# Fewer and larger DMAs for the head sums and the decays of a chunked state-space stage

## The chip, the cores and the metric

One core of one Trainium2 chip runs the whole program in one launch. The metric is the device time of that launch in microseconds. The engines are named as in the profile: PE (TensorE) for matmuls, DVE (VectorE), ACT (ScalarE), POOL (GpSimd), and SP (SyncE), whose queue issues nearly all DMAs.

## What is computed

The program is four layers in a row on `x` of 4 x 512 x 256, each adding to `x` what it makes of a layer norm of `x`: a Mamba scan, a mixture of experts (MoE), a chunked state-space layer (SSD), and the same MoE again. The change touches the SSD layer alone, which is, cut to what matters:

```python
dA  = (dt * A).reshape(b, c, 32, 64)            # 64 heads, 8 numbers each
Acs = jnp.cumsum(dA, axis=2)
Lm  = jnp.exp(_segsum(dA))                      # within a chunk: exp(Acs[l] - Acs[s]), l >= s
Y_diag = einsum('bclhn,bcshn,bchls,bcshp->bclhp', Ch, Bh, Lm, xd)
states = einsum('bclhn,bclh,bclhp->bchpn', Bh, exp(Acs[-1] - Acs), xd)
prev   = scan over chunks: h = h * exp(Acs[-1]) + states
Y_off  = einsum('bclhn,bchpn,bclh->bclhp', Ch, prev, exp(Acs))
y = rms_norm(Y_diag + Y_off) * silu(z) @ W_out
```

`Acs`, the running sums of a head within a chunk of 32 tokens, are the "head sums" (`cs`). `exp(Acs[-1])`, the factor by which a state shrinks over a chunk, are the "decays".

## The kernel before

A program in two parts writes itself. `block` records every operation in a list (`Plan.note`), with its tiles; `Plan.order` then places them: a list scheduler with a price for every operation picks, engine by engine, the ready operation of the highest rank; 24 such orders are made and the one whose replay is shortest is emitted. Every instruction therefore carries line 612 (`emit`) in the profile (table loads carry line 610), and is told apart by the names of its tiles. Each engine runs its instructions in the order emitted and waits where an operand is not ready. So a change to a few DMAs changes the order of the whole program a little.

The SSD layer runs over four batches b of 512 tokens. 16 blocks of 32 tokens make the chunks; the 64 heads are taken in four groups g of 16, a group in four quads q of four heads, and two groups make a pair p. For each batch:

- `front_a` and `front_b` (lines 1507 to 1708) make the projections, the head sums (bank `pcs`, copied to `c_s`), and `over_blocks`, the decays of each head over blocks. Each of the two halves of `c_s` (`a` = 0, 1: 32 heads, each in a high and a low part, 64 rows of 512) is stored to DRAM tensor `cs_rows` (line 1664). The decays go to `dk_rows`, 64 heads of 128 numbers (line 1680). A head's row in `dk_rows` is its decays over 16 blocks, repeated for its 8 numbers.
- `weighted` (lines 1775 to 1799) makes for one group the weighted inputs `xw` and `xe` on POOL, stores `xw` to `x_rows`, and loads the group's head sums back from `cs_rows` into one of four buffers `less`, as rows k (block) by q, h, s: eight DMAs a group, one for each of the two parts and four quads (lines 1791 to 1798).
- `apart` (lines 1801 to 1809) loads `x_rows` back, spread by blocks, into one of two buffers `x_b`, in four DMAs a group.
- `decayed` (lines 1870 to 1884): matmul `pe` of `less` and `c_s`, exponential on ACT, mask on DVE or POOL: tile `m`. `within` (lines 1886 to 1899): 32 x 16 small matmuls `pz` of `m` and `x_b` a group; the group before the one that `decayed` works on.
- `states` (lines 1811 to 1868), once a pair: matmuls `pst` into `starts`, two scans on DVE (one each for h = 0, 1, the half of a group's heads), then matmuls `po_s_p`. Each scan reads a tile `decays` of 128 partitions x 1024: 64 partitions for each group of the pair, each row the same 4 KB of `dk_rows`. It is loaded by two DMAs of 64 partitions, one for each group (lines 1822 to 1825). `decays` has two buffers, so a pair's two loads wait for the scans of the pair before.

All these DMAs are issued on SP, one after another, in the planner's order. SP also waits in that order: an issue whose data is not there holds everything behind it. The DMAs take turns on eight completion semaphores, so that an issue also waits until the DMA eight places ahead has landed.

Of the kernel before, what the change touches and what calls it, by code (L numbers as in the profile page):

```python
# [22 lines left out]
F32 = mybir.dt.float32  # L23
# [15 lines left out]
DI, NH, HD, DS = 512, 64, 8, 64  # L39
# [16 lines left out]
BL, NB = 32, P // 32  # L56
# [14 lines left out]
def bc(ap, axis, n):  # L71

    a = ap.unsqueeze(axis)
    shape = list(a.shape)
    shape[axis] = n
    return a.to_broadcast(shape)
# [641 lines left out]
def block(ctx: ExitStack, tc: Plan, a: dict, out: bass.AP):  # L718
# [929 lines left out]
    def front_b(b):  # L1648

        nm, small, rot, d_a, zs, xs, wt, ld = made_a.pop(b)  # L1650

        pcs = bank(FRONT_BANKS if b == 0 else "mm", f"pcs_{nm}")
        for i in range(NT):
            T.matmul(
                pcs[:, i * P : (i + 1) * P], d_a[:, i].rearrange("p a c h -> p (a c h)"), upto_b,
                start=True, stop=True,
            )
        cs_rows = dram.tile([2, NH, L], F32, tag="cs_rows", name=f"cs_rows_{nm}")
        cs = c_s[b % 2]
        for a in range(2):  # L1660
            src, lo = pcs[a * NH : (a + 1) * NH], a * NH + NH // 2
            S.copy(cs[a][NH:], src)
            V.tensor_tensor(cs[a][NH + NH // 2 :], pcs[lo : lo + NH // 2], cs[a][NH + NH // 2 :].bitcast(F32), ALU.subtract)
            nc.sync.dma_start(out=cs_rows[a], in_=cs[a][NH:].bitcast(F32))
            V.tensor_copy(
                tot[b % 2][a * NH // 2 : (a + 1) * NH // 2, 1:],
                src[: NH // 2].rearrange("p (k l) -> p k l", l=BL)[:, :-1, BL - 1],
            )

        pc = bank(FRONT_BANKS if b == 0 else "mm", f"pc_{nm}")  # L1670
        T.matmul(pc[:, : L // 2], upto_b, d_a[:, :, :, 0, :], start=True, stop=True)
        T.matmul(pc[:, L // 2 :], after_b, d_a[:, :, :, 0, :], start=True, stop=True)
        ends = s_o.tile([P, 2, NT, NH], F32, tag="ends", name=f"ends_{nm}")
        S.activation(ends.rearrange("p c i h -> p (c i h)"), pc, AF.Exp)

        nk = NT * NB
        over_blocks = small("over_blocks", (NH, HD, nk))
        S.activation(over_blocks, bc(tot[b % 2], 1, HD), AF.Exp)
        dk_rows = dram.tile([NH, HD * nk], F32, tag="dk_rows", name=f"dk_rows_{nm}")
        nc.sync.dma_start(out=dk_rows, in_=over_blocks.rearrange("p d k -> p (d k)"))  # L1680
        yield


        nh = NT * NB // 2
        bt = small("rest", (P, L))
        cm = c_m[b % 2]
        for g in range(2):
            pt = bank(FRONT_BANKS if b == 0 else "mm", f"pbc_{nm}_{g}")
            for i in range(NT):
                T.transpose(pt[:, i * P : (i + 1) * P], rot[:, i, g].rearrange("p c n -> p (c n)"), ident)  # L1690
            S.copy(bt if g == 0 else cm, pt)
        bm = b_m[b % 2]
        S.copy(bm, rot[:, :, 0, 0, :])
        gm = s_o.tile([P, nh, 2, BL], F32, tag="gm", name=f"gm_{nm}")
        pg = bank(FRONT_BANKS if b == 0 else "mm", f"pg_{nm}")
        for k in range(nk):
            ks = slice(k * BL, (k + 1) * BL)
            for h in range(4):
                T.matmul(pg[h * BL : (h + 1) * BL, ks], bt[:, ks], cm[:, ks], start=True, stop=True)
        S.activation(gm.rearrange("p j c l -> p (j c l)"), pg, AF.Copy, scale=0.5)  # L1700
        dg = small("tsin", (P, NT, DS))
        V.tensor_tensor(dg, rot[:, :, 0, 0, :], rot[:, :, 1, 0, :], ALU.mult)
        dd = small("dd", (P, NT))
        V.tensor_reduce(dd, dg, AX.X, ALU.add)
        V.tensor_tensor(ld, ld, bc(dd, 2, NH), ALU.mult)
        ready[b] = dict(
            nm=nm, zs=zs, y=xs, wt=wt, ld=ld, ends=ends, dk_rows=dk_rows, gm=gm, cm=cm, bm=bm, cs=cs, cs_rows=cs_rows
        )
# [66 lines left out]
    def weighted(b, g):  # L1775

        c = ready[b]
        nm = f"{c['nm']}_{g}"
        ch, hs = slice(g * P, (g + 1) * P), slice(g * 16, (g + 1) * 16)
        xs = c["y"][:, :, ch]  # L1780
        xw = pool2.tile([P, NT, P], F32, tag="xw", name=f"xw_{nm}", bufs=1)
        G.tensor_tensor(per_head(xw), per_head(xs), bc(c["wt"][:, :, hs], 3, HD), ALU.mult)
        x_rows = dram.tile([L, P], F32, tag="x_rows", name=f"x_rows_{nm}", bufs=4)
        nc.sync.dma_start(out=x_rows.rearrange("(i p) f -> p i f", p=P), in_=xw)
        xe = pool2.tile([P, NT, P], F32, tag="xe", name=f"xe_{nm}", bufs=XE_BUFS)
        G.tensor_tensor(per_head(xe), per_head(xw), bc(c["ends"][:, 1, :, hs], 3, HD), ALU.mult)

        G.tensor_tensor(per_head(xs), per_head(xs), bc(c["ld"][:, :, hs], 3, HD), ALU.mult)
        nk = NT * NB
        ls = less[g]  # L1790
        for part in range(2):
            for q in range(4):
                lo = part * NH // 2 + g % 2 * 16
                src = c["cs_rows"][g // 2, lo + q : lo + 16 : 4, :]
                nc.sync.dma_start(
                    out=ls[part * nk : (part + 1) * nk, q, :].bitcast(F32).rearrange("k (h s) -> k h s", h=4),
                    in_=src.rearrange("h (k s) -> k h s", s=BL),
                )
        units[b, g] = dict(xe=xe, x_rows=x_rows, less=ls)

    def apart(b, g):
# [9 lines left out]
    def states(b, p):  # L1811

        c = ready[b]
        nm = f"{c['nm']}_p{p}"
        nk = NT * NB
        pair = (2 * p, 2 * p + 1)
        half = [slice(h * DS, (h + 1) * DS) for h in range(2)]
        G.memset(starts[:, :, 0], 0.0)
        decays = []
        for h in range(2):  # L1820
            t = pool2.tile([P, P // 2 * nk], F32, tag="decays", name=f"decays_{nm}_{h}")
            for j, g in enumerate(pair):
                at = 16 * g + 8 * h
                src = c["dk_rows"][at : at + 8, :].rearrange("h d -> (h d)")
                nc.sync.dma_start(out=t[half[j]], in_=src.partition_broadcast(DS))
            decays.append(t)


        for r0 in range(0, NB, 2):
            pts = [bank("c", f"pst_{nm}_{r0 + r}", (P, NT, P)) for r in range(2)]  # L1830
            tc.chain = []
            for i in range(NT):
                for r in range(r0, r0 + 2):
                    if i * NB + r + 1 == nk:
                        continue
                    rs = slice(r * BL, (r + 1) * BL)
                    for j, g in enumerate(pair):
                        T.matmul(
                            pts[r - r0][half[j], i, :], c["bm"][rs, i, :], units[b, g]["xe"][rs, i, :],
                            start=True, stop=True,  # L1840
                        )
            tc.chain = None
            for r in range(r0, r0 + 2):
                n = NT if r + 1 < NB else NT - 1
                at = starts[:, :, r + 1 : r + 2 + NB * (n - 1) : NB]
                S.copy(at.rearrange("p c i -> p i c"), pts[r - r0][:, :n, :])
            yield
        for h in range(2):
            at = starts[:, h * P // 2 : (h + 1) * P // 2, :].rearrange("p c k -> p (c k)")
            V.tensor_tensor_scan(at, decays[h], at, 0.0, ALU.mult, ALU.add)  # L1850
        yield
        po = [bank("c", f"po_{nm}_{j}", (P, NT, P)) for j in range(2)]
        tc.chain = []
        for k in range(nk):
            for j in range(2):
                r = slice(k % NB * BL, (k % NB + 1) * BL)
                T.matmul(
                    po[j][r, k // NB, :], c["cm"][half[j], k * BL : (k + 1) * BL], starts[half[j], :, k],
                    start=True, stop=True,
                )  # L1860
        tc.chain = None
        for j, g in enumerate(pair):
            hs = slice(g * 16, (g + 1) * 16)
            off = pool2.tile([P, NT, P], F32, tag="off", name=f"off_{nm}_{j}")
            V.tensor_tensor(per_head(off), per_head(po[j]), bc(c["ends"][:, 0, :, hs], 3, HD), ALU.mult)
            y = c["y"][:, :, g * P : (g + 1) * P]
            G.tensor_tensor(y, y, off, ALU.add)
        yield
# [176 lines left out]
```

## Time and profile before

| | |
|---|---|
| median of 3 runs | 846.15 us (842.12 to 849.16) |
| the profiled execution | 836.37 us, of it 834.7 us from the first to the last instruction |
| busy, share of that span | PE 85%, DVE 82%, ACT 63%, POOL 63% |
| the SSD stage by its batches, us of the span | 440 to 505, 505 to 572, 572 to 640, 640 to 712 |
| DMA share of the 16 engines in these four | 0.42, 0.31, 0.32, 0.57 |
| DMAs in the stage for head sums | 8 stores (2 a batch), 128 loads of 8 KB |
| DMAs in the stage for decays | 4 stores, 32 loads of 256 KB |

The page's table of groups gives an engine's busy time for one operation and its mean; its table of DMA issues gives the number, the size and the median time from issue to landing. The chain of work is followed back from the last instruction of the program: "SPq" in it is time in which the SP queue was issuing a DMA that the chain stood behind.

### The profile page before, as it was taken

The numbers are of one execution on the slowest core, as the hardware profiler recorded it, in microseconds if no ns is written. First come the engines' busy times: TensorE is split into PE (matmuls) and PEld (weight loads), VectorE is DVE, ScalarE is ACT, GpSimd is POOL, SyncE is SP. The second block draws the span as 40 slices with busy tenths as digits, with TensorE's granted clock in tenths as the row PEclk, the third lists the DMA queues.
The fourth block names the chain that finished last, engine by engine and source line by source line (L and its number), as shares of the span: only waits on it lengthen the run. The fifth ranks groups of instructions, "written<-read, shape, count | busy, mean of one in ns | idle before, by whom it ended". The sixth has DMA issues, their size and how long they took to land.

```text
span 834.7 us, 16400 instructions
## 1 busy us (share of the span) xinstructions
PE 709.5 (85%) x6194; PEld 457.5 (55%) x6194; DVE 683.8 (82%) x1278; ACT 523.4 (63%) x965; POOL 527.2 (63%) x410
## 2 busy tenths in 40 slices
PE   8889879966676789799997697789789886999996
PEld 5333324221022247587886475676567664888784
DVE  7488999999999984898996678697677546799987
ACT  2898976865345486566687455645636544686764
POOL 5735857767767574655555886863862873558555
PEclk9989999976577699999999599899789778999999
DMA  8321252241341002600004522521531584000001
GB/s 273 117 76 64 71 184 64 92 162 64 101 176 51 1 7 57 273 1 0 2 5 112 116 64 60 112 65 38 117 80 32 131 264 101 1 1 26 25 2 51
DMA packets 79247, 67.55 MB, mean 81 GB/s; under 512 B 48696, under 2 KB 66040, under 8 KB 78400
## 3 DMA queue, kind: packets, MB, share of 16 engines
q1 hardware_dynamic: 77664, 65.35, 27.2%
q10 hardware_dynamic: 1504, 1.15, 0.5%
q8 instruction: 49, 0.80, 0.4%
q14 instruction: 30, 0.25, 0.1%
HBM read 49.67 MB, written 16.80 MB: 80 GB/s over the span
## 4 chain that ended last, share of the span: by engine, by line
PE 35%; DVE 15%; ACT 8%; SPq 5%; issue 5%; POOL 3%; DMA 1%; POOLq 0%; ACTq 0%; DVEq 0%
PE ph_e L612 8%; PE ph_f L612 6%; SPq L612 5%; PE pz_s L612 4%; DVE hs L612 3%; PE px_s L612 3%; PE po_s L612 2%; DVE starts L612 2%; PE pst_s_p L612 2%; DVE bx L612 1%; PE po_s_p L612 1%; ACT L610 1%; ACT ph_e L612 1%; PE pe_s L612 1%; DVE ph_f L612 1%
## 5 line engine op out<-in xcount | busy, mean ns | idle before, releaser
L612 POOL TENSOR_TENSOR hs<-hs,cb 128x1024 f32<-128x1024 f32 x64 | 151.8, 2380 | 73.8 <-DVE hs L612 61.1
L612 DVE TENSOR_TENSOR_SCAN hs<-da,bx 128x512 f32<-128x512 f32 x128 | 150.5, 1213 | 8.3 <-ACT da L612 5.8
L612 ACT ACTIVATE da<-ds,a_neg 128x512 f32<-128x512 f32 x128 | 87.5, 689 | 76.8 <-DVE hs L612 76.6
L612 PE MATMUL ys<-hs,over 128*32 128x512 f32 x256 | 73.7, 755 | 27.9 <-POOL hs L612 27.9
L612 DVE TENSOR_TENSOR bx<-us,pb 128x1024 f32<-128x1024 f32 x64 | 76.3, 1211 | 0.2
L612 POOL TENSOR_TENSOR m_s<-m_s,gm_s 128x512 f32<-128x512 f32 x32 | 45.3, 1421 | 32.8 <-ACT m_s L612 32.7
L610 ACT ACT_TABLE_LOAD x51 | 65.4, 1283 | 0.9
L612 PE MATMUL pconv<-hh,conv 128*128 128x512 f32 x128 | 60.8, 622 | 1.1 <-ACT hh L612 1.1
L612 ACT ACTIVATE ph_f<-ph_f 128x512 f32<-128x512 f32 x64 | 37.5, 588 | 26.9 <-DVE ph_f L612 26.6
L612 DVE TENSOR_TENSOR ph_f<-ph_f,expert_b 128x512 f32<-128x512 f32 x64 | 43.9, 694 | 11.7 <-DMA expert_b<-in_expert_b_dram 5.7
L612 ACT ACTIVATE ph_e<-ph_e 128x512 f32<-128x512 f32 x64 | 36.8, 586 | 23.7 <-DVE ph_e L612 15.9
L612 PE MATMUL ph_e<-expert_h,xs_of_xh_e 128*128 128x512 f32 x128 | 44.9, 413 | 4.2 <-ACT c_e L612 4.2
L612 PE MATMUL pe_s<-c_s,less 128*128 128x512 f32 x64 | 32.9, 544 | 16.2 <-DMA less<-cs_rows_s 7.4
L612 PEld LDWEIGHTS ys<-hs,over 128*32 128x32 f32 x256 | 8.8, 118 | 66.9 <-POOL hs L612 51.9
L612 POOL TENSOR_TENSOR c_e<-c_e,hb_e 128x512 f32<-128x512 f32 x16 | 20.6, 1290 | 36.1 <-ACT hb_e L612 36.1
L612 PEld LDWEIGHTS pconv<-hh,conv 128*128 128x128 f32 x128 | 24.1, 196 | 34.4 <-issue 28.1
L612 ACT COPY starts<-pst_s_p 128x512 f32<-128x512 f32 (+1 forms) x32 | 29.6, 1010 | 18.3 <-PE pst_s_p L612 18.3
L612 PE MATMUL pz_s<-x_b,m_s 128*32 128x32 f32 x2048 | 31.9, 216 | 10.0 <-DMA x_b<-x_rows_s 5.7
L612 DVE TENSOR_TENSOR_SCAN starts<-decays_s_p,starts 128x1024 f32<-128x1024 f32 x16 | 38.9, 2439 | 1.5 <-issue 1.3
L612 PEld LDWEIGHTS pz_s<-x_b,m_s 128*32 128x32 f32 x2048 | 26.3, 127 | 23.4 <-issue 15.3
L612 PE MATMUL ph_f<-expert_h,xh_f 128*128 128x512 f32 x96 | 38.4, 400 | 0.7 <-ACT c_f L612 0.7
L612 PE MATMUL ph_f<-expert_l,xh_f 128*128 128x512 f32 x96 | 38.4, 400 | 0.0
(399 smaller groups left out, 2163.2 us busy)
## 6 DMA issues: line engine op xcount, KB each, us to landing
decays_s_p<-dk_rows_s SPq DMA_DIRECT2D x32, 256.0 KB, 4.3
ds<-d_rows SPq DMA_DIRECT2D x14, 512.0 KB, 3.8
us<-u_rows SPq DMA_DIRECT2D x14, 512.0 KB, 3.9
cb<-c_rows SPq DMA_DIRECT2D x16, 256.0 KB, 3.3
x_rows_s<-xw_s SPq DMA_DIRECT2D x16, 256.0 KB, 3.0
x_b<-x_rows_s SPq DMA_DIRECT2D x64, 64.0 KB, 2.4
x<-in_x_dram SPq DMA_DIRECT2D x4, 512.0 KB, 4.7
raw_expert<-in_expert_w_dram SPq DMA_DIRECT2D x4, 512.0 KB, 7.1
```

The costliest lines, as they stand in the source:

```text
L610: self.real.scalar.preload_act_table_set(n.table)
L612: n.inst = f(*[self.swap(v) for v in n.args], **{k: self.swap(v) for k, v in n.kw.items()})
```

## The change

The head sums of a half are stored in four DMAs of 16 rows instead of one of 64; within each 16 rows the order in DRAM becomes quad by quad, head by head, which is the order in which `less` wants them. A group's `less` is then loaded by one DMA for each part, 16 blocks x 16 heads = 256 rows of 32 numbers, instead of four of 64 rows. A pair's decays for one h come by one DMA for both groups instead of two.

```diff
-            nc.sync.dma_start(out=cs_rows[a], in_=cs[a][NH:].bitcast(F32))
+            for at in range(0, NH, 16):
+                nc.sync.dma_start(
+                    out=cs_rows[a, at : at + 16].rearrange("(q h) l -> h q l", h=4),
+                    in_=cs[a][NH + at : NH + at + 16].bitcast(F32),
+                )
...
         for part in range(2):
-            for q in range(4):
-                lo = part * NH // 2 + g % 2 * 16
-                src = c["cs_rows"][g // 2, lo + q : lo + 16 : 4, :]
-                nc.sync.dma_start(
-                    out=ls[part * nk : (part + 1) * nk, q, :].bitcast(F32).rearrange("k (h s) -> k h s", h=4),
-                    in_=src.rearrange("h (k s) -> k h s", s=BL),
-                )
+            lo = part * NH // 2 + g % 2 * 16
+            nc.sync.dma_start(
+                out=ls[part * nk : (part + 1) * nk].bitcast(F32).rearrange("k q (h s) -> k (q h) s", s=BL),
+                in_=c["cs_rows"][g // 2, lo : lo + 16, :].rearrange("h (k s) -> k h s", s=BL),
+            )
...
-            for j, g in enumerate(pair):
-                at = 16 * g + 8 * h
-                src = c["dk_rows"][at : at + 8, :].rearrange("h d -> (h d)")
-                nc.sync.dma_start(out=t[half[j]], in_=src.partition_broadcast(DS))
+            src = c["dk_rows"].rearrange("(g c h) d -> g c (h d)", c=2, h=8)[2 * p : 2 * p + 2, h]
+            nc.sync.dma_start(out=t, in_=bc(src, 1, DS))
             decays.append(t)
```

As the built programs have it, outermost dimension first: a load of decays had 64 rows of 1024 on both sides, the source with a step of zero; now its destination is 128 rows of 1024 and its source is 2 x 64 (a step of zero) x 1024. A load of `less` was 16 x 4 x 32 and is 16 x 16 x 32. A store of head sums was 64 x 512 on both sides; now its source is 16 x 512 and its destination 4 x 4 x 512.

## The prediction

> **What bounds the kernel now.** I read the page's chain first, then the chain cut to the SSD stage, its waits, and the DMA tables. The chain's share for SP stands out, since SP computes nothing:
>
> ```profile
> PE 35%; DVE 15%; ACT 8%; SPq 5%; issue 5%; POOL 3%; DMA 1%; POOLq 0%; ACTq 0%; DVEq 0%
> ```
>
> The chain cut to 440 to 712 us puts the whole of it into the stage that is changed, 16.6% of 272 us = 45 us, and cut to 577 to 606 us it is nearly alone:
>
> ```profile
> by line: SPq L612 80.9%; DMA x_b<-x_rows_s 8.5%; issue 7.8%; PE pe_s L612 2.5%; PE pz_s L612 1.2%
> ```
>
> There SP issues DMA after DMA (the timeline of SP), some 0.5 us each, until the fourth `x_b` of group 2 has gone at 602.5:
>
> ```profile
> 586.00 3.87 SPq L612 DMA_DIRECT2D less<-cs_rows_s  x6
> 589.98 1.96 SPq L612 DMA_DIRECT2D x_b<-x_rows_s  x4
> 591.99 2.39 SPq L612 DMA_DIRECT2D less<-cs_rows_s  x3
> 594.42 1.11 SPq L612 DMA_DIRECT2D decays_s_p<-dk_rows_s  x2
> 595.62 0.53 SPq L612 DMA_DIRECT2D x_rows_s<-xw_s  x1
> 596.20 2.02 SPq L612 DMA_DIRECT2D less<-cs_rows_s  x4
> 598.26 1.09 SPq L612 DMA_DIRECT2D decays_s_p<-dk_rows_s  x2
> 599.40 1.32 SPq L612 DMA_DIRECT2D less<-cs_rows_s  x1
> 600.82 2.21 SPq L612 DMA_DIRECT2D x_b<-x_rows_s  x4
> ```
>
> What PE pays is read from the stage's waits on PE (total, times, longest):
>
> ```profile
> PE pe_s L612 <- DMA less<-cs_rows_s: 7.4, 4, 5.8
> PE pz_s L612 <- DMA x_b<-x_rows_s: 5.7, 3, 2.9
> ```
>
> 13.1 us in all; the rest of the 45 us runs beside PE, which is busy for 222 of the 272. Then the DMAs themselves (number, KB, median us from issue to landing):
>
> ```profile
> decays_s_p<-dk_rows_s SPq DMA_DIRECT2D x32, 256.0 KB, 4.3
> x_rows_s<-xw_s SPq DMA_DIRECT2D x16, 256.0 KB, 3.0
> x_b<-x_rows_s SPq DMA_DIRECT2D x64, 64.0 KB, 2.4
> less<-cs_rows_s SPq DMA_DIRECT2D x128, 8.0 KB, 2.8
> ```
>
> Two more rows carry the forecast. `less` landed in 2.7 us at the median and 14.3 at most (minimum, median, maximum):
>
> ```profile
> DMA to landing us min/median/max: 1.6/2.7/14.3
> ```
>
> The late ones were issued from 667 on, behind two 2 MB loads of expert weights (665.55 and 666.59): a transfer waits for what was queued on the same DMA engines before it. And a stretch in which these loads keep all 16 busy gives the rate of one (columns end with DMA share and GB/s):
>
> ```profile
> 669.00:677.00 8.00, 7.90 (x127) 6.24 (x114) 4.71 (x8) 4.32 (x9) 7.84 (x9) 1.00 1.01 397
> ```
>
> 397 / 16 = 24.8 GB/s for one engine.
>
> **The change part by part.** *Loads of head sums, 128 to 32.* A load of `less` holds SP for 0.6 us on average (the timeline's 77.3 us for 128). 64 rows or the 512 rows of an `x_b` cost SP about the same (medians 0.43 and 0.49), so one of 256 does too; landing 2.4 to 2.8 by the same two rows. *Stores, 8 to 32*, at 0.47: 24 more. *Loads of decays, 32 to 16*, at 0.57. Together 88 issues fewer, some 50 us of the queue's time, between 0 us (all beside other work) and 45 us (all that the chain shows) of the program's. I take the 13.1 us that PE waited: the nearest row, since PE's order is fixed and it pays only when it stands.
>
> *How a load of decays is spread.* It moves 512 KB now, and its source has 2 as the outermost dimension. The trace keeps every update of a DMA's semaphore. All DMAs of SP have 16, which I read as one for each engine that took part, but two: `raw_bias` and `bias`, the only ones of 4 rows, have five: for `raw_bias` one as the issue ends (24.15 us) and four at landing (25.05, 25.07, 25.14, 25.37). So a DMA of 4 rows ran on 4 engines, while those with 16, 32 or 64 outermost ran on 16. No row has 128 on one side and 2 on the other. Bounds: 16 engines, landing as now, 4.3 us; 2 engines, 256 KB each at 24.8 GB/s = 10.6 us, and 21.2 for a pair's two if they use the same two engines. I take the second: the nearest row is the one with a small outermost dimension. The stores (destination 4 x 4) would run on 4 engines with four rows of 2 KB each, as many per engine as 64 rows on 16: nothing.
>
> *The Trainium skill*, "DMA: Bandwidth & Descriptors", "Rules for kernel authors", speaks on both sides: it tells one to coalesce many small transfers, and it says that an outermost dimension below 16 on either side confines the DMA to at most that many engines. By the first alone the time would be 833 us; by the second, which gives two engines here, 890. The five updates agree with the second.
>
> *What stands behind the decays.* Every other DMA of SP has rows on those two engines and waits for its share there, as `less` did for 14.3 us. In the order of the built program, in batches 1 and 2 a pair's first two loads stand ahead of `x_b` of group 1 (in batch 2 also of its `x_rows`). Batch 2, counted from its first store of head sums (574.8 before): 20 issues at 0.5 put the first load at +10, with the two engines taken from about +11 to +32. `x_rows` of group 1 lands at +33; four issues and 2.4 us put `x_b` at +37.5, where it was +19.7. `xw` has one buffer, so `x_rows` of group 2 follows then: issue +35.5, landing 3.0, four issues, 2.4: +43, where PE had it at 605.1, +30.3. **13 us late**, and PE's matmuls behind it stand in fixed order. Batch 1: the decays cannot go before `dk_rows` (issued at 523.4, +18, behind ACT) has landed, +20; engines taken to +42; `x_rows` of group 2, issued meanwhile, lands at about +43.5, `x_b` at +48 for 537.7, +32.3: **16 late**. Batch 0: the second load stands just ahead of the first `x_b`: 10.6 us on its two engines, less 3, since seven loads of `less` stood around that `x_rows` (458.2 to 463.5 us) and two do now: **7**. Batch 3 (from 643.3): the second pair's two loads stand ahead of `x_b` of group 2, and wait for the first pair's scans, which ended at 668.5, +25, and come 21 later; so they take the engines from +47 to +68, and that `x_b` lands at +69 for +50 (691.3 and 2.4); against these 19 the late `less` of group 3 goes (PE's wait of 5.8 us), as all `less` now go ahead of or between the expert weights: **13**. In each batch PE stands at `pz`; behind it in PE's order are the last quads' `pe`, `pst`, `po_s_p` and the next batch's projections, and DVE, ACT and POOL wait for these. Sum 49 us, with the gain on SP already in it as it is counted by issues. Off it go 5 us for waits of PE that end while it stands anyway (PE idles 10 to 14 us in each batch).
>
> *The scans.* The two scans of a pair came 12 to 39 us after its first load was issued; the second load would land at 23. The short ones are first pairs, which are later anyway; nothing added.
>
> *The order of the rest.* In Mamba and the first MoE the built orders differ in places; DVE is busy for 232 of the 240 us from 50 to 290, so a better order has little to win and I take 0, with 4 us either way.
>
> Sum: 836.4 + 49 - 5 = 880 us for an execution like the profiled one. The median of the runs stands 9.8 us above that execution, so the forecast is **890 us**.
>
> **Rivals.** *A, the loads use all 16 engines.* For: 128 destination rows. Against: the 4-row DMAs. Then only SP's gain is left: 846 - 13 = 833 us, faster. It decides at about 3 us of exposed delay a batch, which is decays landing in some 6 us instead of 4.3, six engines or more.
>
> *B, two engines, but only the scans wait.* If other DMAs pass the two busy engines, the second scan of each pair stands only where its load lands after 23 us: the distances were 24, 39, 20.5, 22.6, 22, 22, 12 and 23, so 17 us, less 13: 850 us. Against: the 14.3.
>
> *C, the blocks are exposed in full.* If nothing covers the first pairs' 21.2 us and each second pair holds back some 5: 4 x 26 - 13 = 91: 937 us. For: within a batch PE has little to do that needs no `x_b`. Against: 10 to 14 us of idle PE a batch.
>
> *D, the queue is not relieved*, because the eight completion semaphores hold SP instead: a part of C.
>
> **How the numbers follow.** Forecast 0.62, A 0.13, B 0.10, C with D 0.15. The forecast's own range is 861 (846 + 24.5 - 5 - 4: half of the 49 covered, and the order's 4) to 931 (846 + 73.5 - 5 + 17: half as much again, and the scans). With B and C the range is 850 to 940. A and the tails, 2 in 10, are left out. 1% is about what a measurement of this kernel can tell from no change: faster A, 0.12; within 1% most of B, 0.08; slower 0.80.
>
> **What would show it.** Right: decays land in 12 to 25 us; the DMA share falls while PE waits for `x_b` for 10 us or more a batch; `x_b` or `x_rows` land in over 10 us after the decays; SPq nearly gone from the chain of issues that follow one another, with DMA in its place; the stage's 272 us become some 315. Wrong: decays land in 4 to 6 us (A), or land late while `x_b` keeps 2.4 us (B).

## The result, and the profile after

| | before | after |
|---|---|---|
| median of 6 runs each | 844.31 us (839.11 to 849.16) | 912.51 us (906.92 to 917.16) |
| ratio, 95% interval | | 1.080 (1.0745 to 1.086) |
| profiled execution, its span | 836.37, 834.7 us | 914.04, 912.3 us |
| DMAs in the stage for head sums and decays | 136 and 36 | 64 and 20 |
| mean granted TensorE clock | 0.894 | 0.844 |

The change made the kernel 68 us slower. The forecast was 890 us, in a range of 850 to 940. The page's chain of the kernel after, by engine:

```profile
PE 34%; DMA 11%; DVE 10%; POOL 8%; issue 5%; ACT 4%; SPq 3%; POOLq 0%; DVEq 0%; ACTq 0%
```

Against the chain shown of before, SP's queue fell from 5% to 3%, DMA rose from 1% to 11% and POOL from 3% to 8%. The chain cut to the stage, of before (440 to 712 us) and of after (440 to 800 us), names the DMAs:

```profile
by line: SPq L612 16.6%; PE pz_s L612 10.7%; issue 8.0%; PE px_s L612 5.8%; PE po_s L612 5.4%; DVE starts L612 5.1%; PE pst_s_p L612 4.9%; PE po_s_p L612 4.2%; PE pe_s L612 3.2%; PE ph_f L612 2.0%; DMA x_b<-x_rows_s 1.8%; DVE m_s L612 1.7%;
by line: DMA x_rows_s<-xw_s 15.3%; issue 9.3%; DMA decays_s_p<-dk_rows_s 9.1%; SPq L612 7.9%; PE pz_s L612 5.0%; POOL m_s L612 4.8%; DVE starts L612 4.6%; PE px_s L612 3.0%; POOL zs_s L612 2.9%; PE pst_s_p L612 2.6%; PE pe_s L612 2.2%; DVE 
```

24% of 360 us are two kinds of transfers that are not among the costliest parts of the chain before: the stores `x_rows` and the loads of decays. SP's queue in the stage's chain went from 45 to 28 us. What the engines waited for in the same window (total, times, longest), first PE, then POOL, then DVE:

```profile
PE pz_s L612 <- DMA x_b<-x_rows_s: 44.7, 4, 17.4
PE pyt_s L612 <- POOL zs_s L612: 17.3, 1, 17.3
PE pz_s L612 <- POOL m_s L612: 11.9, 6, 5.7
```

```profile
POOL xw_s L612 <- DMA x_rows_s<-xw_s: 63.8, 6, 20.9
```

```profile
DVE starts L612 <- DMA decays_s_p<-dk_rows_s: 12.3, 3, 9.0
```

The prediction had PE pay through `x_b`, which is the largest line. It used the one buffer of `xw` to delay the next `x_rows`, but it did not count what else POOL holds back meanwhile. POOL stood 64 us (4.7 before) because `xw` has one buffer and the next `xw` needs the store of the last one landed.

Batch 0 as SP issued it (start, time, what, how many):

```profile
463.83 0.56 SPq L612 DMA_DIRECT2D decays_s_p<-dk_rows_s  x1
...
465.00 0.38 SPq L612 DMA_DIRECT2D x_rows_s<-xw_s  x1
...
474.03 0.52 SPq L612 DMA_DIRECT2D decays_s_p<-dk_rows_s  x1
477.91 7.79 SPq L612 DMA_DIRECT2D x_b<-x_rows_s  x4
485.81 3.35 SPq L612 DMA_DIRECT2D x_rows_s<-xw_s  x1
...
491.26 2.57 SPq L612 DMA_DIRECT2D x_b<-x_rows_s  x4
```

The landings are read from the updates of each DMA's semaphore. The first load of decays, issued at 463.83, landed 12.88 us later, at 476.7. `x_rows`, issued 1.2 us behind it, had 14 of its 16 updates within 3.1 us and the last two at 12.8 and 12.9. The second load (474.03) landed after 15.32 us, at 489.35; the first `x_b`, issued at 477.91, had 14 of 16 within 2.2 us and the last two at 11.7 and 11.9. Two parts of sixteen were late each time, as many as the engines of the decays.

SP's queue was held as well. Of the four `x_b` at 477.91 the third took SP 5.44 us to issue (479.74), where 0.49 is usual, although the DMA eight places ahead of it had landed at 477.2; in batch 1 two such issues, at 546.30 and 555.86, took 9.5 and 5.2 us with no wait for a semaphore in them:

```profile
543.76 17.85 SPq L612 DMA_DIRECT2D x_b<-x_rows_s  x4
```

What holds an issue is not shown. From a batch's first store of head sums to the end of the last `pz`, SP's issues took 141 us for 267 DMAs before and 175 us for 179 after, of which 12.9 us were a wait for PE. In batch 0 this lies on the chain: the `x_rows` at 485.81 could go only when the four `x_b` had been issued.

The chain in batch 2 shows what the late parts cost. There a store waits behind both loads of its pair, and the second pair's second scan behind its load:

```profile
621.47 2.52 POOL m_s L612 x2
623.99 22.01 DMA x_rows_s<-xw_s
646.13 1.07 POOL xw_s L612
...
671.40 2.25 DVE starts L612
673.67 15.63 DMA decays_s_p<-dk_rows_s
689.32 2.29 DVE starts L612
```

The stage in the parts of its four batches (length, then busy time of PE, PEld, DVE, ACT, POOL with counts, granted clock, DMA share, GB/s):

```profile
451.00:529.00 78.00, 51.37 (x838) 37.78 (x836) 49.74 (x87) 35.87 (x68) 46.84 (x38) 0.74 0.31 82
529.00:609.00 80.00, 58.64 (x1128) 45.03 (x1128) 53.96 (x83) 36.71 (x69) 39.81 (x34) 0.83 0.23 59
609.00:697.00 88.00, 62.39 (x1039) 46.47 (x1039) 48.76 (x78) 39.58 (x73) 40.06 (x34) 0.82 0.21 56
697.00:782.00 85.00, 52.85 (x1129) 41.70 (x1129) 31.44 (x57) 30.12 (x52) 35.96 (x33) 0.66 0.41 129
```

PE was busy for 225 us of these 331, as it was for 221 of the 270 before: the stage holds nearly the same work and 57 us more of standing. The DMA engines are busy for 21 to 31% in the first three batches (31 to 42% before) while PE waits for DMA: a mean over 16 engines does not show that two of them are full.

### The profile page after: what moved, and what is told of

Read it like the earlier page. It is cut to its first block, busy times and chain, and to the rows that moved or that the text cites. A ratio compares the mean times of both kernels' runs of the same rounds, so it can differ in the third digit from the quotient of the medians.

```text
span 912.3 us, 16289 instructions
## 1 busy us (share of the span) xinstructions
PE 735.2 (81%) x6194; PEld 472.9 (52%) x6194; DVE 683.7 (75%) x1278; ACT 516.2 (57%) x959; POOL 524.4 (57%) x410
## 4 chain that ended last, share of the span: by engine, by line
PE 34%; DMA 11%; DVE 10%; POOL 8%; issue 5%; ACT 4%; SPq 3%; POOLq 0%; DVEq 0%; ACTq 0%
PE ph_e L612 10%; PE ph_f L612 9%; DMA x_rows_s<-xw_s 6%; DMA decays_s_p<-dk_rows_s 4%; SPq L612 3%; PE pz_s L612 2%; DVE hs L612 2%; POOL m_s L612 2%; DVE starts L612 2%; PE px_s L612 2%; DVE bx L612 1%; PE po_s L612 1%; POOL zs_s L612 1%; PE pst_s_p L612 1%; PE ys L612 1%
## 5 line engine op out<-in xcount | busy, mean ns | idle before, releaser
L612 PE MATMUL pz_s<-x_b,m_s 128*32 128x32 f32 x2048 | 33.0, 222 | 57.5 <-DMA x_b<-x_rows_s 44.7
L612 POOL TENSOR_TENSOR m_s<-m_s,gm_s 128x512 f32<-128x512 f32 x32 | 42.0, 1323 | 46.0 <-ACT m_s L612 46.0
L612 POOL TENSOR_TENSOR xw_s<-xs_s,wt_s 128x512 f32<-128x512 f32 x16 | 17.7, 1106 | 85.3 <-DMA x_rows_s<-xw_s 63.8
L612 DVE TENSOR_TENSOR m_s<-pe_s,gm_s 128x512 f32<-128x512 f32 x32 | 21.8, 683 | 43.9 <-PE pz_s L612 36.1
L612 ACT ACTIVATE ph_f<-ph_f 128x512 f32<-128x512 f32 x64 | 37.2, 590 | 21.6 <-DVE ph_f L612 21.2
```

Of the source, the lines that this page charges most:

```text
L612: n.inst = f(*[self.swap(v) for v in n.args], **{k: self.swap(v) for k, v in n.kw.items()})
```

## The experiments

Lengths of batches below go from a batch's first store of head sums to the next one's, the last to the end of the last `pz`, each from the trace of one execution.

**Only one thing changed: on how many engines a load runs.** The kernel before, with the source of its 64-row loads of decays written as 2 x 32, 4 x 16 or 8 x 8 (steps of zero). Number, size and order of the instructions stay.

```diff
-                nc.sync.dma_start(out=t[half[j]], in_=src.partition_broadcast(DS))
+                nc.sync.dma_start(out=t[half[j]], in_=bc(bc(src, 0, 32), 0, 2))
```

> The kernel before with one thing changed: the source of each load of decays (64 rows with a step of zero) is written as 2 x 32 with steps of zero. Every engine's order of instructions, the number of DMAs and their bytes (32 loads of 256 KB) stay as they are. Theory (engines as many as the outermost dimension): each load runs on two engines, 128 KB each at 24.8 GB/s, 5.3 us and 21 for the four of a pair on the same two, so nearly the whole loss comes: 885 to 930 us. Rival (order of the program, size of a load, number of DMAs): 838 to 848 us, as before.

> The same with 4 x 16 as the source: four engines, 64 KB each, 2.6 us a load and 10.6 for a pair's four. Theory: the block is half as long and part of it is hidden: 850 to 875 us. Rival: 838 to 848 us.

> The same with 8 x 8 as the source: eight engines, 32 KB each, 1.3 us a load, 5.3 for a pair's four. Theory: a load lands in some 4 to 6 us, and what is left is hidden: 840 to 852 us. Rival: 838 to 848 us, which this run alone does not tell apart; it is for where the loss begins.

| source of a load | 64 (before) | 8 x 8 | 4 x 16 | 2 x 32 |
|---|---|---|---|---|
| time, us | 839.3 | 850.4 | 865.9 | 914.4 |
| ratio, 95% interval | 1 | 1.014 (1.009 to 1.018) | 1.034 (1.028 to 1.040) | 1.090 (1.085 to 1.095) |
| updates of its semaphore | 16 | 9 | 5 | 3 |
| landing, us: minimum, median, maximum | 3.3, 4.2, 7.7 | 4.2, 5.9, 9.8 | 5.5, 8.6, 12.7 | 8.8, 13.7, 23.2 |
| lengths of the batches, us | 68.7, 69.4, 68.5, 63.5 | 76.4, 70.0, 71.7, 66.0 | 75.8, 76.0, 75.0, 70.0 | 86.4, 83.9, 86.8, 90.0 |

This is the run that settles the cause. With every engine's order as before, the form of a source alone brings 75 us, and the loss grows as the engines become fewer. The updates are one more than the engines: with 2, 4 and 8 outermost one update comes as the issue ends, the others at landing. The Trainium skill, "DMA: Bandwidth & Descriptors", "Why a DMA increments its semaphore by 16 and not by 1", says the same: the issuing queue writes the missing part at once, and each engine that takes part adds one as its data lands; the counts 3, 5 and 9 agree. In batch 0 the four loads of the first pair, issued within 1.8 us, landed 9.1, 14.3, 19.8 and 25.0 us after the first was issued: steps of 5.2, 5.5 and 5.1 us, against 5.3 worked out from 128 KB at 24.8 GB/s. They use the same two engines, one behind the other. On four engines the four loads landed 3.3, 2.5 and 2.6 us apart (64 KB at that rate take 2.6). On eight it was 2.2, 2.8 and 2.1, where 32 KB would take 1.3: there the rate of an engine no longer gives the step, and what does is not shown. The chain of the 2 x 32 kernel, cut to the stage (436 to 784 us):

```profile
by line: DMA decays_s_p<-dk_rows_s 26.3%; issue 7.1%; SPq L612 6.7%; DMA x_rows_s<-xw_s 5.7%; PE pz_s L612 4.4%; DMA expert_l<-kept_expert_l 3.8%; DMA moe_rows<-kept_rows 3.5%; DVE starts L612 2.8%; PE pe_s L612 2.5%; PE px_s L612 2.1%; PE 
```

**Either part of the change alone.** Head sums as changed with the decays in two loads again, and the decays as changed with the head sums as before:

```diff
-            src = c["dk_rows"].rearrange("(g c h) d -> g c (h d)", c=2, h=8)[2 * p : 2 * p + 2, h]
-            nc.sync.dma_start(out=t, in_=bc(src, 1, DS))
+            for j, g in enumerate(pair):
+                at = 16 * g + 8 * h
+                src = c["dk_rows"][at : at + 8, :].rearrange("h d -> (h d)")
+                nc.sync.dma_start(out=t[half[j]], in_=src.partition_broadcast(DS))
```

> The head sums' part of the change alone: stores by quads and one load of 256 rows for four of 64, while the decays keep two loads of 64 partitions. Theory (the two-engine decays cost all of it): the gain on SP is left, at most the 13.1 us that PE waited and what of the 45 us of SP's queue more: 815 to 840 us, ratio to before 0.97 to 0.995. Rival (the new order of the program, its later start of the SSD stage by 14.8 us, or the stores on four engines make it slow): 860 to 915 us, and batches of the stage as long as with the whole change.

Measured 830.5 us, ratio 0.987 (0.983 to 0.992): 1.3% below the kernel before, a small gain but clear of the noise, and the shortest time of this study.

> The decays' part of the change alone: one load of 512 KB for a pair and h, source 2 x 64 x 1024; head sums as before. Theory (two engines, and other transfers behind them): slower about as much as the whole change, +50 to +85 us, 895 to 930 us, as SP is relieved of only 16 issues; decays land 12 to 22 us after their issue and x_b behind them. Rival (order of the program or the stores): 840 to 850 us.

Measured 926.8 us, ratio 1.102 (1.0975 to 1.106), loads landing in 12.1 to 22.2 us. The two ratios multiply to 1.088 beside 1.080 for the whole: the parts hardly act on each other. The Trainium skill has a rule for this very edit ("DMA: Bandwidth & Descriptors", "Rules for kernel authors"): of two transfers to disjoint halves of the partitions it would make one over 128. Here that cost 86 us (0.102 of 841.3), because the one transfer had 2 as its source's outermost dimension; the page's rule on that dimension is the one that decided. In the kernel with the head sums alone, what PE waited for over its whole stage:

```profile
PE pz_s L612 <- DMA x_b<-x_rows_s: 2.4, 2, 1.4
...
PE pe_s L612 <- DMA less<-cs_rows_s: 2.2, 1, 2.2
```

Before, these two lines were 5.7 and 7.4 us.

**One load for both groups, on sixteen engines.** The decays are written to DRAM in eight copies, so that the source of the 512 KB load is 16 x 8 (step of zero) x 1024:

```diff
-        nc.sync.dma_start(out=dk_rows, in_=over_blocks.rearrange("p d k -> p (d k)"))
+        for g in range(4):
+            nc.sync.dma_start(
+                out=dk_rows[g].rearrange("r h d -> h r d"),
+                in_=bc(over_blocks[16 * g : 16 * g + 16].rearrange("p d k -> p (d k)"), 1, 8),
+            )
...
-            nc.sync.dma_start(out=t, in_=bc(src, 1, DS))
+            nc.sync.dma_start(out=t, in_=bc(src, 1, 8))
```

> The whole change, but the decays of a pair and h are written to DRAM in eight copies, so that the one load of 512 KB has 16 as the outermost dimension of its source (16 x 8 with a step of zero x 1024) and the number of DMAs for loading stays at 16. The four stores of copies (128 rows each) are added per batch. Theory (the number of engines decides): 16 engines, 815 to 845 us, decays landing in 4 to 6 us. Rival (the size of 512 KB, or one DMA where there were two, makes the wait): 890 to 915 us, as with the change.

Measured 844.8 us, ratio 1.003 (0.9995 to 1.006); loads land in 4.5, 5.1 and 10.5 us (minimum, median, maximum). The size of a load and the number of loads are not what costs 8%. It stays 14 us above the head sums alone, and why was not settled: twelve more stores, loads that land 0.6 us later and another order of the whole program came together.

**The decays on another queue.** ACT issues them instead of SP, still on two engines:

```diff
-            nc.sync.dma_start(out=t, in_=bc(src, 1, DS))
+            nc.scalar.dma_start(out=t, in_=bc(src, 1, DS))
```

> The whole change, but the decays' loads are issued on ACT's queue instead of SP's; they still run on two engines. Two ways in which others can stand behind them: if a transfer waits only behind what its own queue put on the same engine, x_rows and x_b on SP's queue pass the decays, and what is left is the scans' wait and sharing of two engines: 840 to 875 us. If any transfer on the two engines waits whatever queue it came by: 890 to 920 us.

Measured 901.4 us, ratio 1.073 (1.066 to 1.081). That is in the range of the second expectation, but neither has the mechanism. Four loads `x_b` that SP issued beside decays that ACT issued at 566.95 and 572.51:

```profile
570.10 1.90 SPq L612 DMA_DIRECT2D x_b<-x_rows_s  x4
```

The four landed at 580.0, 585.3, 590.7 and 591.4, each with 14 of 16 updates within 3.6 us of its issue and two late; the decays landed at 580.7 and 591.2. A DMA of one queue does not stand behind the whole of what the other has queued: the two took turns. But it came off badly. An `x_b` has 32 rows of 128 bytes on each engine, and 32 rows of 4 KB, as the decays have them, take 128 KB / 24.8 GB/s = 5.3 us: the steps of 5.3 and 5.4 us to the second and the third are those of one small row for each large one. The first, 9.9 us from issue to landing, does not fit that count, so by what rule the two take turns is not shown. For the program the second queue changes little: its interval overlaps that of the change.

This run also tells what SP's held queue is worth. Here SP's issues in the stage took 109 us for 163 DMAs, and none of the decays' issues on ACT took more than 1.2 us. The queue is nearly relieved, and 7.3% of loss stays, so the hold is not the main cost.

**Which pair's loads cost.** The 2 x 32 source in the loads of first pairs only, then of second pairs only:

```diff
+                nc.sync.dma_start(out=t[half[j]], in_=bc(bc(src, 0, 32), 0, 2) if p == 0 else src.partition_broadcast(DS))
```

> The kernel before with the two-engine source (2 x 32) only in the loads of each batch's first pair; those of the second pair stay on 16 engines. With both it was 914 us, 75 more. By the prediction's steps the first pairs carry batches 0, 1 and 2 (7, 16 and 13 of 49) and the second pairs batch 3 (13): some three quarters, +50 to +60 us, 890 to 900. Rival (a pair's block costs the same wherever it stands): about half, +33 to +42, 872 to 882 us.

> The same in the loads of the second pair only. By the prediction's steps one quarter and the scans: +13 to +25 us, 853 to 865. Rival (the same for both pairs): +33 to +42, 872 to 882 us.

Measured 908.1 us, ratio 1.080 (1.074 to 1.086) for the first pairs, and 853.2 us, 1.016 (1.009 to 1.023), for the second. Lengths of the batches, less those of before: 16.9, 20.7, 16.1 and 15.4 us for the first pairs; -0.3, 2.0, 3.3 and 9.5 for the second. The first pairs carry five sixths, and in every batch; they cost more than the steps gave (890 to 900), and the second pairs as much as the low end of theirs. The rival of equal shares falls.

**POOL's wait.** The whole change with two buffers for `xw`; for the room, two for `xe` instead of three:

```diff
-XE_BUFS = 3
+XE_BUFS = 2
...
-        xw = pool2.tile([P, NT, P], F32, tag="xw", name=f"xw_{nm}", bufs=1)
+        xw = pool2.tile([P, NT, P], F32, tag="xw", name=f"xw_{nm}", bufs=2)
```

> The whole change, but two buffers for xw instead of one, so that POOL's next xw does not wait for the store of x_rows (it waited 63.8 us on it in the stage). For the room one of the three buffers of xe goes. Theory (POOL, in order, holds m and zs behind that wait, and PE behind these): some 15 to 30 us come back, 882 to 898 us. Rival (x_b must wait for the same store anyway, so the matmuls stand as long): 905 to 920 us.

Measured 900.1 us, ratio 1.074 (1.067 to 1.081), between the two and not told apart from the whole change's 1.080 (1.0745 to 1.086). The same exchange with the head sums' part alone is its control:

> The head sums' part alone (830.5 us, ratio 0.987) with two buffers for xw and two for xe instead of one and three: what the exchange of buffers is worth by itself, without the two-engine loads. If the 12 us by which the exchange differed under the whole change come from the exchange: 815 to 822 us. If they came from fewer stalls behind the two-engine loads, or from the order alone: 828 to 840 us.

Measured 841.5 us, ratio 1.000 (0.997 to 1.003), in neither of the expected ranges: the exchange by itself costs 11 us there. With the whole change and two buffers, POOL's wait for `x_rows` is down from 63.8 to 1.7 us, yet the batches last 77.5, 78.3, 86.6 and 86.9 us, in sum 329 against 331 without it. What PE waits for:

```profile
PE pz_s L612 <- DMA x_b<-x_rows_s: 50.8, 6, 13.4
PE po_s_p L612 <- DVE starts L612: 17.1, 5, 9.6
PE pe_s L612 <- DMA less<-cs_rows_s: 9.8, 4, 4.9
```

PE's own wait for `x_b` is 50.8 us where it was 44.7. In every batch one `x_rows` still landed 13 to 22 us after its issue, and `x_b` needs it. How much of the loss goes by way of POOL is not settled: by the ratios the two-engine loads cost 7.4% with two buffers (1.074 against 1.000) and 9.4% with one (1.080 against 0.987), some 16 us less, by the sums of the batches 64 against 71 us, and the exchange moved `xe` and the order as well. Most of the loss stays without POOL's wait.

## Why the prediction was right, and where it was wrong

- *How a load of decays is spread: right.* Two engines, 10.6 us a load, 21.2 for two. In the trace a pair's first load lands after 12.5 us at the least, of which some 2 are there for any transfer; and the second of batch 1's first pair landed 10.6 us after the first (553.8 and 564.4).
- *What stands behind the decays: right in kind, 27 us too small.* `x_rows` and `x_b` waited with two of their sixteen parts, and PE behind them. By batch, with the SP gain in it as the prediction had it, by how much further behind each batch ends than the one before it (in sum 76 before rounding, of the spans' 78; the medians differ by 68, since the profiled execution of before was 8 us faster than its median and that of after 1.5 us slower):

| batch | 0 | 1 | 2 | 3 |
|---|---|---|---|---|
| predicted, us | 7 | 16 | 13 | 13 |
| measured, us | 24 | 11 | 20 | 22 |
| 2 x 32 in the first pair's loads alone | 16.9 | 20.7 | 16.1 | 15.4 |
| 2 x 32 in the second pair's loads alone | -0.3 | 2.0 | 3.3 | 9.5 |

- *The step that failed is the cover of the first pairs.* For batch 0 it counted one load of 10.6 us, less 3; for batch 3 it counted the second pair only. The timeline of batch 0 shows why: `x_rows` stood behind the first load, and only then could `x_b` go, which stood behind the second. A store and the load that needs it pay in turn, so both loads are paid for. In batch 3 the fourth `x_b`, issued 1.3 us behind the first pair's first load, landed after 12.5 us, and the second load (712.29) stood ahead of the four `x_b` at 720.31, which landed after up to 10.6. Two engines alone made the batches 17.7, 14.5, 18.3 and 26.5 us longer, 19 in the mean: between the 15 a batch of the forecast (its 49 and the 13 of SP, over four) and the 26 of rival C.
- *Some of the closeness is luck.* The forecast added 9.8 us from a profiled execution to the median. For the kernel after that step is -1.5 us. Execution against execution the change cost 78 us where 44 were forecast; the 890 stands only 22 us from the median of 912.5 because the 9.8 us made up for part of this. And batch 1 was put 5 us too high while the other three were 7 to 17 too low.
- *The 5 us taken off for waits that vanish: no run shows them.* PE waits for other things in their place, 17.3 us in one piece for POOL's `zs`.
- *SP's gain: right.* 13.1 us predicted from PE's own waits, 10.6 measured (1 - 0.9874 of 841.3), with 8.5 us of these waits gone. How near the two are may be luck too: the eight copies and the exchange of buffers, neither with a load on two engines, put the time 14 and 11 us above that of the head sums alone. The 45 us of SP in the chain were no measure of it: a chain follows the issues whatever runs beside them.
- *The stores on four engines, "nothing": not quite.* They landed in 2.0 us (2.3 before), but a store takes SP 0.60 us at the median instead of 0.46, with 24 more of them. In the head sums alone it is inside the 10.6. Two sums of the prediction are off without consequence: at its own costs the 88 issues are 55 us, not 50, and rival B's waits are 16 us, not 17.
- *The scans, "nothing added": wrong by little.* DVE waited 12.3 us in three places for decays, 9.0 of them in one.
- *The order of the rest, 0 +- 4:* the first store of head sums came at 451.5 instead of 436.7. With the eight copies it came at 450.8, and batch 0 ended only 4 us after that of before: a shorter batch gave the late start back. By that, some 19 of the 24 us of batch 0 are the loads.
- The rivals: A (16 engines) fell with the first landing. B (only scans wait) fell with `x_b`. D (the queue not relieved) came true in part: SP's issues took 34 us more in all, for 88 fewer, but the completion semaphores did not hold the long ones shown above. In the kernel with 2 x 32 sources, whose issues are as many as before, they do hold SP, in total, times and longest:

```profile
SPq L612 <- DMA decays_s_p<-dk_rows_s: 34.5, 13, 5.2
```

- Of the signs named beforehand these came: landings of 12 to 29 us, a lower DMA share, `x_b` and `x_rows` late after decays, DMA at the head of the stage's chain. SP did not nearly go from it: 28 us are left of 45. The stage lasted 331 us, not 315.

## What to carry to other kernels

Before two DMAs are made one, look at the outermost dimension of both sides as the instruction carries it: a broadcast or a pair of groups put first can confine a large transfer to a few engines, and the price is less that transfer's own landing than every other transfer with a part on those engines. Count the block once for each step of a chain of dependent transfers that starts inside it, since a store and the load that needs it pay one after the other. And take the gain of fewer issues from what the bound engine itself waits for, not from the share of the issuing queue in the chain.

## What the runs showed of the hardware

- A DMA on k engines, fewer than sixteen, has k + 1 updates of its semaphore (3, 5 and 9 for 2, 4 and 8), one as the issue ends. With it the number of engines is read from a trace.
- Loads on two engines go to the same two: four of them landed 5.1 to 5.5 us apart, with 14 other engines there. On four engines the steps were 2.5 to 3.3 us, which fits the same four.
- Behind loads on two engines SP's issue of another DMA took up to 9.5 us (0.49 at the median for an `x_b`), with no wait for a semaphore in it.
- Eight engines were not enough to be free: 1.014 (1.009 to 1.018), though a load landed only 1.7 us later at the median.
- A store of head sums with destination 4 x 4 x 512 held SP for 0.60 us against 0.46 for one of 64 x 512. That the four engines are the reason is not shown: loads on two or four took SP 0.51 to 0.52 us against 0.57.
- Two queues share an engine in turn, and the one with small rows comes off badly: beside decays from the other queue `x_b` of 64 KB landed 5.3 and 5.4 us after one another, where one lands in 2.4 us from its issue in the kernel before.
- The granted clock was 0.894 over the span before and 0.844 after, and 0.66 in the last batch, where PE was busy for 53 of 85 us; PE's busy time in the stage rose only from 221 to 225 us.
